# Layer 0's rounds: one bounded product of factors for the decays in six of eight rounds, and dt's chain taken apart over a slot

## The chip, the cores and the metric

The kernel runs on one core of a Trainium2 chip. The core has a matrix engine (TensorE, PE in the profile; its weight loads are listed as PEld), a vector engine (VectorE, DVE), a scalar engine for activations (ScalarE, ACT), a general one (GpSimd, POOL) and queues for DMAs (here mostly SyncE's, SP). Each engine executes its instructions in order; an instruction waits on semaphores for what it needs from other engines. The metric is the device time in microseconds, the median of several runs.

## The reference, cut to what matters

The kernel computes four layers on an input of 8 sequences x 512 tokens x 128 features. Only the mixer of layer 0 is touched. It is a selective state-space recurrence whose inputs depend on the step before:

```python
def step(carry, inp):
    state, y_prev = carry
    xBC_t, dt_t, z_t = inp
    xBC = silu(xBC_t + y_prev @ W_rxbc.T)
    dtr = silu(dt_t + y_prev @ W_rdt.T)
    ...
    dt = jax.nn.softplus(dtr + dt_bias).astype(jnp.float32)
    dA = jnp.exp(dt * A)
    ...
    state = state * dA[:, :, None, None] + dt[:, :, None, None] * x_h[:, :, :, None] * B_hn[:, :, None, :]
    y = (state * C_hn[:, :, None, :]).sum(-1) + D_param[None, :, None] * x_h
    y = y.reshape(B, D_SSM)
    g = y * silu(z_t)
    ...
    yn = (gg * jax.lax.rsqrt(ms + EPS)).reshape(B, D_SSM) * norm_w
    out_t = yn @ W_out.T
    return ((state, yn), out_t)
```

There are 4 heads of 64 features, and the state is 128 wide. `A` is negative, so each step lets the state decay by `exp(dt * A)`. Layer 0 also has an expert network (8 experts, each for all tokens, one chosen per token); it does not depend on the mixer.

## The kernel before, in words

**Rounds.** The step's dependence on `y_prev` is resolved by iteration: `ROUNDS` = 8 times the whole sequence is computed in parallel from the last round's `yn`. A round of one sequence is a `Unit` (k, b), so there are 64 units, k outermost. A unit has four tiles c of 128 tokens. In round 0 the raw inputs come from the convolution (16 matmul passes a tile, L157, and z, L166); they are stored to DRAM (`xd`, and z as `zd`) and fetched again in later rounds (L141, L146), where the feedback product (8 passes, L161) is added (L169). After the last round, `apart_still` compares rounds 6 and 7 (largest difference against 5e-5, `CLOSE`); if they differ by more, a loop over `again` computes more rounds, each unit by itself. In the profiled execution that loop is not entered: L169 runs 224 times, 7 rounds of 8 units of 4 tiles.

**Slots.** `run` writes the order out by hand under a manual schedule, and each engine keeps that order. Slot i works on four units at once: `new` (unit i, its inputs), `mid` (unit i-1, silu, dt, the turn of B and C and their pair products), `old` (unit i-2, products, outputs) and `last` (unit i-3, its last output and its norm). There are 67 slots of four chunks. Two calls of `fill` in each chunk add expert work: one of them usually four hidden matmuls (`ph`, L609, then four Relus on ACT, L622), the other four output matmuls (`po`, L591, then an add on DVE one call later, L630). Their number per chunk does not depend on the units.

**One unit.** At the start of a slot, ACT loads the silu table (L126), does one silu over all four tiles (L176), and loads the table with exp and ln. Then comes dt's chain: v and nv on DVE (L192, L193), exp on ACT (L194), e1 (L195), ln (L196), and d, l, dt, da (L197 to L200). PE forms running sums and totals of da (L203, L204), and ACT their exponentials `ec`. For the decays between two tokens of a tile, POOL multiplies the triangle by da for each head (`span`, L211, 128x512), PE sums over it (`pseg`, L225), ACT takes the exponential (`E`, L229), and DVE multiplies it with the masked pair products `gm` to `M` (L253, L234). PE then needs four products a tile, one for each head's own `M` (L260), the part from the carried state (L262) and, but for the last tile, the tile's own state (L265). POOL also makes `xdt`, `xp` and `xw` (L219, L221, L237). DVE forms the state and the outputs (L275 to L291); ACT squares them for the norm (L292); PE turns them (L298) and ACT copies them to `gT` (L299), which feeds the next round.

**PSUM.** There are pools of one bank or two: `pre`, a shared tile "b" (pc, pbc, pz and pr take turns in it), `pseg`, `py`, and a shared tile "s" (pds and pgt); two more banks are the experts'.

Of the kernel before, what the change touches and what calls it, by code (L numbers as in the profile page):

```python
# [55 lines left out]

CW = 516
HW = CW // 2
ROUNDS = 8
CLOSE = 5e-5  # L60
SILU, EXPLN = "silu_and_others", "natural_log_exp_and_others"


class Unit:
    def __init__(self, k, b):
        self.k, self.b = k, b
        self.bc, self.gm, self.xd, self.xp, self.e, self.m, self.r = {}, {}, {}, {}, {}, {}, {}
        self.py, self.ps, self.s = {}, {}, {}


class Recurrence:

# [3 lines left out]
    def __init__(self, tc, ctx, keep, K, I, dr, xnT, spare, B, T):  # L76
# [5 lines left out]
        self.psA, self.psB, self.psG = pool("pa", 1, space=PSUM), pool("pb", 1, space=PSUM), pool("pg", 1, space=PSUM)  # L82
        self.psY, self.psS = pool("py", 1, space=PSUM), pool("ps", 1, space=PSUM)
# [13 lines left out]
        tri = load("tri", [P, 4, P])  # L97
        self.upto, self.after, self.shift, self.carry = (tri[:, i, :] for i in range(4))
# [9 lines left out]
        WcT = self.un.tile([P, 4, CW], F32, name="ux")[:, 0, :]  # L108
# [4 lines left out]
        self.spare = spare  # L113
# [6 lines left out]
        self.apart = wp.tile([P, B], F32, name="apart")  # L120
        self.xd = [dr.tile([P, 4, CW], F32, name=f"xd{b}") for b in range(B)]
        self.zd = [dr.tile([P, 4, 256], F32, name=f"zd{b}") for b in range(B)]
        self.yd = [dr.tile([P, 4, 256], F32, name=f"yd{b}") for b in range(B)]
# [14 lines left out]
    def fetch(self, u):  # L138
        u.x = self.un.tile([P, 4, CW], F32, name="ux")
        for c in range(self.NC if u.k else 0):  # L140
            self.nc.sync.dma_start(out=u.x[:, c, :], in_=self.xd[u.b][:, c, :])  # L141

    def fetch_gate(self, u):
        u.z = self.un.tile([P, 4, 256], F32, name="uz")
        if u.k:
            self.nc.sync.dma_start(out=u.z, in_=self.zd[u.b])  # L146

    def inputs(self, u, c):

        nc = self.nc  # L150
        pre = self.psA.tile([P, 2, 512], F32, name="pre")
# [10 lines left out]
        x = self.halves(u.x[:, c, :])  # L162
        if u.k == 0:
            nc.vector.tensor_tensor(x, pre[:, :, 0:HW], self.halves(self.convb), ALU.add)
            pz = self.psB.tile([P, 512], F32, name="pz", tag="b")
            nc.tensor.matmul(pz[:, 0:256], self.xnT[:, u.b, c * P + 3 : c * P + 3 + P], self.WzT, start=True, stop=True)  # L166
            nc.vector.tensor_copy(u.z[:, c, :], pz[:, 0:256])
        else:
            nc.vector.scalar_tensor_tensor(x, pre[:, :, 0:HW], self.rs[:, u.b, c : c + 1], x, ALU.mult, ALU.add)  # L169

    def silu(self, u):
        nc = self.nc
        if u.k == 0:
            nc.sync.dma_start(out=self.xd[u.b], in_=u.x)
        self.tables(SILU)
        nc.scalar.activation(u.x, u.x, AF.Silu)  # L176
        if u.k == 0:
            nc.scalar.activation(u.z, u.z, AF.Silu)
            nc.sync.dma_start(out=self.zd[u.b], in_=u.z)
        self.tables(EXPLN)  # L180

    def small(self, name, n=4):
        return self.sm.tile([P, 4, n], F32, name=name)

    def dt(self, u):

        nc = self.nc
        tt, stt = nc.vector.tensor_tensor, nc.vector.scalar_tensor_tensor
        four = lambda t: t.rearrange("p (c h) -> p c h", c=4)
# [18 lines left out]
    def spans(self, u, c):  # L208

        u.r[c] = self.wk.tile([P, 4, P], F32, name="span")  # L210
        self.nc.gpsimd.tensor_tensor(  # L211
            u.r[c], self.upto.unsqueeze(1).to_broadcast([P, 4, P]), u.da[:, c, :].unsqueeze(2).to_broadcast([P, 4, P]), ALU.mult
        )
# [203 lines left out]

# [1089 lines left out]
```

## Time and profile before

| what | value |
|---|---|
| runs of the kernel before | 4888.32, 4879.22, 4885.47 us; median 4885.47 us |
| the profiled execution: its time | 4862.31 us |
| its span, first to last instruction | 4860.5 us |
| mean granted TensorE clock | 0.911 |
| busy over the span | PE 3921.8 us (81%), DVE 2433.7, ACT 2148.3, POOL 1682.9 us |
| first matmul of layer 0's rounds (L157) | at 77.27 us |
| last matmul of the last unit's norm (L312) | at 2880.81 us |
| sums of da (L203) of slots 1, 3, 8, 49, 51, 59, 64 | at 115.57, 201.59, 444.75, 2123.92, 2206.04, 2561.06, 2804.69 us |

The times of L203 mark the slots, since it stands once at the start of each. Slots 3 to 7 take 48.6 us on average ((444.75 - 201.59) / 5), slots 8 to 48 take 40.96, slots 51 to 58 take 44.4, slots 59 to 63 take 48.7 us. In the rows of the timeline below, the first number is the start, the second the duration in us; a pair of brackets holds the idle time of the engine before it and what ended it. A matmul of fp32 shows as two records, and its duration contains the pipeline's latency, so the work of a group is read from one start to the next.

### The profile page before, as it was taken

Reading aid. Unit: us, or ns where it says so; the run is one execution under the profiler, and the core shown is the slowest. Engines: PE = TensorE matmul, PEld = TensorE weight load, DVE = VectorE, ACT = ScalarE, POOL = GpSimd, SP = SyncE. Lnnn points to the kernel's source line nnn. Section 1 sums busy time; section 2 is a strip of 40 time slices with the busy share of each in tenths; the row PEclk is TensorE's granted clock in tenths of the full one; section 3 lists DMA queues with packets and bytes.
Section 4 is the critical chain, followed back from the end, with each engine's and each line's share of the span. In section 5 each row is a group of like instructions: output and inputs, shape, how many; then the busy total and the mean of one; then the engine's idle time right before and its main releaser. Section 6 shows DMA issues by size and latency. Waiting matters only on the chain. (4 is left out here: it accounts for less than half of the span.)

```text
span 4860.5 us, 74671 instructions
## 1 busy us (share of the span) xinstructions
PE 3921.8 (81%) x27702; PEld 2869.4 (59%) x27702; DVE 2433.7 (50%) x7179; ACT 2148.3 (44%) x5067; POOL 1682.9 (35%) x2097
## 2 busy tenths in 40 slices
PE   6877777777777777777777766769999897999998
PEld 5666666666666666666565554225555555666666
DVE  4334444444444444444444545647777336777781
ACT  1333444444444444443333323336666224666675
POOL 1222333333333333332332331630000345777782
PEclk7999999999999999998888888769999898999999
DMA  3001111111111111111111113100000510000000
GB/s 105 36 31 48 44 40 42 42 40 44 40 39 43 35 37 41 39 44 48 53 59 40 51 31 69 52 0 2 2 2 2 106 36 21 2 2 2 2 2 18
DMA packets 85732, 169.07 MB, mean 35 GB/s; under 512 B 10860, under 2 KB 28528, under 8 KB 84210
## 3 DMA queue, kind: packets, MB, share of 16 engines
q1 hardware_dynamic: 80796, 160.22, 11.0%
q8 instruction: 223, 3.65, 0.3%
q10 hardware_dynamic: 4566, 3.99, 0.3%
q14 instruction: 147, 1.20, 0.1%
HBM read 139.50 MB, written 24.68 MB: 34 GB/s over the span
## 5 line engine op out<-in xcount | busy, mean ns | idle before, releaser
L253 DVE TENSOR_TENSOR gm<-pbc,w_tri 128x128 f32<-128x128 f32 x256 | 74.7, 292 | 1002.2 <-PE pbc L251 1002.2
L237 POOL TENSOR_TENSOR xw<-xdt,E 128x256 f32<-128x256 f32 x192 | 119.4, 622 | 1302.6 <-ACT E L229 1295.0
L622 ACT ACTIVATE hid<-ph,be 128x128 f32<-128x128 f32 x1024 | 291.9, 368 | 578.0 <-PE ph L609 578.0
L1196 POOL TENSOR_SCALAR gp<-toe,ng 128x207 f32<-128x207 f32 (+1 forms) x512 | 490.8, 967 | 107.0 <-DVE mn L885 73.0
L898 PE MATMUL pt<-ident,sb 128*128 128x128 f32 x3328 | 497.3, 283 | 13.3 <-ACT pT L901 8.6
L161 PEld LDWEIGHTS pre<-w_Wr,gT 128*128 128x128 f32 x1792 | 378.0, 211 | 190.7 <-issue 141.0
L898 PEld LDWEIGHTS pt<-ident,sb 128*128 128x128 f32 x3328 | 356.2, 141 | 208.8 <-ACT pT L903 78.6
L161 PE MATMUL pre<-w_Wr,gT 128*128 128x258 f32 x1792 | 468.4, 408 | 0.0
L885 DVE CUSTOM_DVE_ANT_0 sb<-ps_s,gp 128x512 f32<-128x512 f32 x512 | 324.1, 685 | 100.5 <-PE ps_s L877 82.8
L901 ACT COPY pT<-pt 128x512 f32<-128x512 f32 (+3 forms) x512 | 255.5, 499 | 243.5 <-PE pt L898 242.1
L229 ACT ACTIVATE E<-pseg 128x512 f32<-128x512 f32 x256 | 152.9, 597 | 451.9 <-PE pseg L225 451.9
L211 POOL TENSOR_TENSOR span<-w_tri,da 128x512 f32<-128x512 f32 x256 | 276.8, 1082 | 217.2 <-PE pseg L225 145.4
L891 ACT ACTIVATE sb<-sb,mn 128x512 f32<-128x512 f32 (+3 forms) x512 | 330.5, 646 | 21.9 <-DVE mn L885 16.5
L225 PE MATMUL pseg<-span,w_tri 128*128 128x512 f32 x512 | 332.6, 737 | 0.0
L591 PE MATMUL po<-ew,hid 128*128 128x128 f32 x2048 | 284.5, 284 | 58.3 <-DVE xn L630 58.3
L203 PE MATMUL pc<-da,w_tri 128*128 128x16 f32 x128 | 38.9, 384 | 354.5 <-DVE da L200 354.5
L591 PEld LDWEIGHTS po<-ew,hid 128*128 128x128 f32 x2048 | 261.5, 200 | 62.0 <-DVE xn L630 61.3
L609 PEld LDWEIGHTS ph<-x,ew 128*128 128x128 f32 x2048 | 279.0, 198 | 15.5 <-ACT hid L622 1.2
L169 DVE SCALAR_TENSOR_TENSOR ux<-pre,rs,ux 128x516 f32<-128x516 f32 x224 | 168.1, 750 | 237.2 <-PE pre L161 237.2
L609 PE MATMUL ph<-x,ew 128*128 128x128 f32 x2048 | 280.2, 282 | 1.0 <-ACT hid L622 1.0
L292 ACT ACTIVATE y<-g 128x256 f32<-128x256 f32 x256 | 106.2, 415 | 361.6 <-DVE g L291 361.6
L260 PE MATMUL py<-xdt,M 128*128 128x64 f32 x2048 | 264.7, 273 | 0.0
(343 smaller groups left out, 8211.2 us busy)
## 6 DMA issues: line engine op xcount, KB each, us to landing
ux<-xd SPq DMA_DIRECT2D x224, 258.0 KB, 3.9
uz<-zd SPq DMA_DIRECT2D x56, 512.0 KB, 5.6
cB<-dc SPq DMA_DIRECT2D x16, 1024.0 KB, 14.1
xd<-ux SPq DMA_DIRECT2D x8, 1032.0 KB
wu<-in_f_up_dram SPq DMA_DIRECT2D x9, 512.0 KB
wd<-in_f_down_dram SPq DMA_DIRECT2D x9, 512.0 KB, 4.2
x<-in_u_dram SPq DMA_DIRECT2D x16, 256.0 KB, 5.3
zd<-uz SPq DMA_DIRECT2D x8, 512.0 KB, 2.6
```

Of the source, the lines that this page charges most:

```text
L161: nc.tensor.matmul(pre[:, h, 0:HW], g, self.W[:, f, cols], start=(f == 0), stop=(f == 1))
L211: self.nc.gpsimd.tensor_tensor(u.r[c], self.upto.unsqueeze(1).to_broadcast([P, 4, P]), u.da[:, c, :].unsqueeze(2).to_broadcast([P, 4, P]), ...
L225: self.nc.tensor.matmul(pg.rearrange("p h t -> p (h t)"), self.after, u.r.pop(c).rearrange("p h t -> p (h t)"), start=True, stop=True)
L260: nc.tensor.matmul(py[:, 0, 64 * h : 64 * h + 64], m[:, h, :], u.xd[c][:, h, :], start=True, stop=True)
L591: self.nc.tensor.matmul(self.po[:, r], hid[:, f, :], w2[:, f, :], start=(f == 0), stop=(f == 3))
L609: self.nc.tensor.matmul(self.ph[:, f, :], self.w[n][0][:, f * P : (f + 1) * P], self.xhT[:, i * P : (i + 1) * P], start=True, stop=True)
L622: self.nc.scalar.activation(self.hid[n][:, f, :], self.ph[:, f, :], AF.Relu, bias=self.be[:, self.jobs[n][0], f : f + 1])
L885: nc.vector.tensor_tensor_reduce(out=sb[:, 0:L], in0=ps[:, g, 0:L], in1=bias[g], scale=1.0, scalar=3.0e38, op0=ALU.add, op1=ALU.min, accum ...
L891: nc.scalar.activation(sb[:, 0:L], sb[:, 0:L], AF.Exp, scale=-1.0, bias=mn)
L898: nc.tensor.transpose(pt[:, j * P : (j + 1) * P], sb[:, j * P : (j + 1) * P], self.ident)
L901: nc.scalar.copy(t[:, 0:L], pt[:, 0:L])
L1196: nc.gpsimd.tensor_scalar(t[:, k0:k1], toe[:, h, o : o + k1 - k0], gates[b][:, i, h : h + 1], None, ALU.mult)
```

## The change

Six rounds (k below `EXACT` = 6) no longer build a matrix of decays for each head. They use two factors for each token instead: `exp` of the sum of da since the middle of the tile, and its inverse. The sums are made with two new matrices, `mid` (the triangle less one half) and `halves_` (one half everywhere); da is bounded at -16 and the sums at 72 either way (`STEEP`, `FAR`). The inverse factor and dt are multiplied onto x (`xs`), the factor onto the gate z (`zf`), and one matmul for all heads with the bare `gm` replaces four; the state's product accumulates into the same PSUM columns. `span`, `pseg`, `E`, `M` and `xw` are then not made. Rounds 6 and 7 keep the sums of their own.

In all rounds, the silu is done tile by tile from the second chunk of the slot before (the third where `mid` is exact), with the table loads there and at the slot's start. dt's chain is split (`dt_begin`, `dt_log`, `dt_end`, `sums`, `factors`) over the first two chunks. The products of `old` open a chunk, and the fetches go tile by tile. D and the gate are multiplied once in round 0 (`dz`, stored and fetched like z), so that an output is one product and one sum. B and C are copied from PSUM by one instruction. The scaling of rounds 6 and 7 for the comparison goes from DVE to POOL; the comparison is of squares summed over a token's 256 features against `CLOSE` squared, one ACT instruction a tile. If it fails, 10 rounds of `again` start from nothing. The PSUM tiles are allocated once, and several results share a bank (`pb`, `pt`, and by turns `py` and `pg`).

In the cut diff below only the added lines are shown, but for the first two; what they take the place of are the functions of the same names in the kernel above, and `dt`, which is split.

```diff
-ROUNDS = 8
+ROUNDS, EXACT = 8, 6
 CLOSE = 5e-5
+STEEP, FAR = -16.0, 72.0
...
+        self.pre = ps.tile([P, 2, 512], F32, name="pre")
+        self.pb, self.pt, self.py, self.pg = (ps.tile([P, 512], F32, name=n) for n in ("pbc", "pt", "py", "pseg"))
...
+        self.upto, self.after, self.shift, self.carry, self.mid, self.halves_ = (tri[:, i, :] for i in range(6))
...
+    def fetch(self, u, c):
+        if u.k:
+            self.nc.sync.dma_start(out=self.ux[u.n % 3][:, c, :], in_=self.xd[u.b][:, c, :])
     def fetch_gate(self, u):
+        u.dz = self.un.tile([P, 4, 256], F32, name="dz", bufs=2)
         if u.k:
+            u.z = self.un.tile([P, 4, 256], F32, name="uz")
             self.nc.sync.dma_start(out=u.z, in_=self.zd[u.b])
+            self.nc.sync.dma_start(out=u.dz, in_=self.dzd[u.b])
...
+    def collect(self, u, c):
+        nc = self.nc
+        pre = self.pre[:, :, 0:HW]
+        if u.k == 0:
+            u.raw = self.wk.tile([P, CW], F32, name="span")
+            nc.vector.tensor_tensor(self.halves(u.raw), pre, self.halves(self.convb), ALU.add)
+            nc.sync.dma_start(out=self.xd[u.b][:, c, :], in_=u.raw)
+            nc.vector.tensor_copy(u.z[:, c, :], self.pt[:, 256:512])
         else:
+            x = self.halves(u.x[:, c, :])
+            nc.vector.scalar_tensor_tensor(x, pre, self.rs[:, u.b, c : c + 1], x, ALU.mult, ALU.add)
+            u.raw = u.x[:, c, :]
+    def silu(self, u, c):
+        nc = self.nc
+        nc.scalar.activation(u.x[:, c, :], u.raw if u.k == 0 else u.x[:, c, :], AF.Silu)
...
+    def skip(self, u, c):
         if u.k == 0:
...
+            self.nc.gpsimd.tensor_tensor(u.dz[:, c, :], u.z[:, c, :], self.Dx, ALU.mult)
+            if c == self.NC - 1:
+                self.nc.sync.dma_start(out=self.dzd[u.b], in_=u.dz)
...
+    def dt_begin(self, u):
+        nc = self.nc
+        u.v, u.nv, u.ex = (self.small(n) for n in ("v", "nv", "ex"))
+        four = lambda t: t.rearrange("p (c h) -> p c h", c=4)
+        nc.vector.tensor_tensor(four(u.v), u.x[:, :, 256:260], four(self.dtb), ALU.add)
+        nc.vector.scalar_tensor_tensor(u.nv, u.v, -1.0, u.v, ALU.mult, ALU.min)
+        nc.scalar.activation(u.ex, u.nv, AF.Exp)
...
+    def dt_log(self, u):
+        nc = self.nc
+        u.e1, u.l = self.small("e1"), self.small("l")
+        nc.vector.tensor_scalar(u.e1, u.ex, 1.0, None, ALU.add)
+        nc.scalar.activation(u.l, u.e1, AF.Ln)
...
+    def dt_end(self, u):
         nc = self.nc
         tt, stt = nc.vector.tensor_tensor, nc.vector.scalar_tensor_tensor
...
+        d = self.small("d")
+        u.dt, u.da = self.small("dt"), self.small("da", bufs=3)
+        stt(d, u.e1, -1.0, u.ex, ALU.add, ALU.subtract)
+        tt(u.l, u.l, d, ALU.subtract)
+        stt(u.dt, u.v, 0.0, u.l, ALU.max, ALU.add)
+        tt(u.da, u.dt, self.A, ALU.mult)
+        if not u.exact:
+            nc.vector.tensor_scalar(u.da, u.da, STEEP, None, ALU.max)
+    def sums(self, u):
+        nc = self.nc
+        pc = u.pc = self.pb[:, 384:432]
+        for i, w in enumerate((self.upto, self.K["ones"], self.after) if u.exact else (self.mid, self.halves_)):
+            nc.tensor.matmul(pc[:, 16 * i : 16 * i + 16], w, u.da, start=True, stop=True)
...
+    def factors(self, u):
+        nc = self.nc
+        u.ec, w = self.small("ec", 48, bufs=3), self.small("w")
+        u.bd = self.small("bd", bufs=3)
+        if u.exact:
+            nc.scalar.activation(u.ec, u.pc, AF.Exp)
+            nc.vector.tensor_tensor(u.bd, u.ec[:, 32:48], u.dt, ALU.mult)
+            return
+        cl = self.small("cl", 32)
+        nc.vector.tensor_scalar(cl, u.pc[:, 0:32], FAR, -FAR, ALU.min, ALU.max)
+        nc.scalar.activation(u.ec[:, 0:32], cl, AF.Exp)
+        nc.scalar.activation(w, cl[:, 0:16], AF.Exp, scale=-1.0)
+        nc.vector.tensor_tensor(u.bd, w, u.dt, ALU.mult)
...
+    def scaled(self, u, c):
+        tt = self.nc.gpsimd.tensor_tensor
+        x = u.x[:, c, 0:256]
+        t = lambda name: self.wk.tile([P, 256], F32, name=name, bufs=2)
+        four = slice(4 * c, 4 * c + 4)
+        u.xs[c] = t("xs")
+        tt(self.heads(u.xs[c]), self.heads(x), self.over((u.dt if u.exact else u.bd)[:, four]), ALU.mult)
+        if not u.exact:
+            u.zf[c] = t("zf")
+            tt(self.heads(u.zf[c]), self.heads(u.z[:, c, :]), self.rate(u, 0, c), ALU.mult)
+        elif c + 1 < self.NC:
+            u.xw[c] = t("zf")
+            tt(self.heads(u.xw[c]), self.heads(x), self.over(u.bd[:, four]), ALU.mult)
+        u.xz[c] = t("xz")
+        tt(u.xz[c], x, u.dz[:, c, :], ALU.mult)
     def spans(self, u, c):
...
+        if u.exact:
+            u.r[c] = r = self.wk.tile([P, CW], F32, name="span")[:, 0:512].rearrange("p (h t) -> p h t", h=4)
+            da = u.da[:, 4 * c : 4 * c + 4].unsqueeze(2).to_broadcast([P, 4, P])
+            self.nc.gpsimd.tensor_tensor(r, self.upto.unsqueeze(1).to_broadcast([P, 4, P]), da, ALU.mult)
     def decays(self, u, c):
...
+        if u.exact:
+            self.nc.tensor.matmul(self.pg, self.after, u.r.pop(c).rearrange("p h t -> p (h t)"), start=True, stop=True)
+            u.m[c] = self.taps[:, c, 0:512]
+            self.nc.scalar.activation(u.m[c], self.pg, AF.Exp)
     def weighted(self, u, c):
...
+        if u.exact:
+            m = u.m[c].rearrange("p (h t) -> p h t", h=4)
+            self.nc.vector.tensor_tensor(m, m, u.gm.pop(c).unsqueeze(1).to_broadcast([P, 4, P]), ALU.mult)
...
+    def turn(self, u, c):
+        nc = self.nc
+        for i in range(2):
+            nc.tensor.transpose(self.pb[:, i * P : (i + 1) * P], u.x[:, c, 260 + i * P : 260 + (i + 1) * P], self.K["ident"])
+        u.bc[c] = self.wk.tile([P, 256], F32, name="bc", bufs=5)
+        nc.scalar.copy(u.bc[c], self.pb[:, 0:256])
...
+    def pairs(self, u, c):
+        nc = self.nc
+        nc.tensor.matmul(self.pb[:, 256:384], u.bc[c][:, 0:P], u.bc[c][:, P:256], start=True, stop=True)
...
+    def masked(self, u, c):
+        u.gm[c] = self.wk.tile([P, P], F32, name="gm", bufs=5)
+        self.nc.vector.tensor_tensor(u.gm[c], self.pb[:, 256:384], self.upto, ALU.mult)
...
+    def products(self, u, c):
+        nc = self.nc
+        cT = u.bc.pop(c)[:, P:256]
+        xs = u.xs.pop(c)
+        bank = self.py if u.exact or c % 2 == 0 else self.pg
+        u.py[c], u.ps[c] = bank, (self.pt[:, 256:512] if u.exact else bank[:, 256:512])
         if c + 1 < self.NC:
...
+            nc.tensor.matmul(u.ps[c], u.x[:, c, 260:388], u.xw.pop(c) if u.exact else xs, start=True, stop=True)
+        if u.exact:
+            m = u.m.pop(c)
+            for h in range(4):
+                e = slice(64 * h, 64 * h + 64)
+                nc.tensor.matmul(bank[:, e], m[:, h * P : h * P + P], xs[:, e], start=True, stop=True)
+            if c:
+                nc.tensor.matmul(bank[:, 256:512], cT, u.s[c], start=True, stop=True)
+            return
+        nc.tensor.matmul(bank[:, 0:256], u.gm.pop(c), xs, start=True, stop=(c == 0))
         if c:
+            nc.tensor.matmul(bank[:, 0:256], cT, u.s[c], start=False, stop=True)
+    def state(self, u, c):
+        if c + 1 == self.NC:
+            return
...
+        u.s[c + 1] = s = self.wk.tile([P, 256], F32, name="S", bufs=2)
+        if u.exact:
...
+        if c:
+            tt(s, u.s[c], ps, ALU.add)
+        tt(heads(s), heads(s if c else ps), self.rate(u, 1, c), ALU.mult)
+        tt(heads(s), heads(s), self.rate(u, 1, c + 1), ALU.mult)
+    def outputs(self, u, c):
...
+        bank = u.py.pop(c)
         y = self.wk.tile([P, 256], F32, name="y", bufs=2)
+        if not u.exact:
...
+            tt(y, bank[:, 0:256], u.zf.pop(c), ALU.mult)
         else:
...
+            if c:
+                tt(self.heads(y), self.heads(bank[:, 256:512]), self.rate(u, 0, c), ALU.mult)
+                tt(y, y, bank[:, 0:256], ALU.add)
+            tt(y, y if c else bank[:, 0:256], u.z[:, c, :], ALU.mult)
+        tt(u.g[:, c, :], y, u.xz.pop(c), ALU.add)
...
+    def norm(self, u):
+        nc = self.nc
+        pr = self.pb[:, 448:452]
...
+        if u.k >= EXACT:
+            self.root(self.rt[:, u.b, :], u.ms[:, 1:5])
+            for c in range(self.NC):
+                rt = self.rt[:, u.b, c : c + 1].to_broadcast([P, 256])
+                nc.gpsimd.tensor_tensor(self.yn[:, c, :], u.g[:, c, :], rt, ALU.mult)
+            if u.k > EXACT:
+                self.compare(u)
+            nc.sync.dma_start(out=self.yd[u.b], in_=self.yn)
...
+    def recall(self, u):
+        if u.k > EXACT:
+            self.nc.sync.dma_start(out=self.was, in_=self.yd[u.b])
...
+    def compare(self, u):
+        nc = self.nc
         for c in range(self.NC):
...
+            w = self.was[:, c, :]
+            nc.vector.tensor_tensor(w, w, self.yn[:, c, :], ALU.subtract)
+            nc.scalar.activation(w, w, AF.Square, accum_out=self.apart[:, u.b, c : c + 1])
...
+            new, mid, old, last, nxt = at(i), at(i - 1), at(i - 2), at(i - 3), at(i + 1)
+            tile = lambda c: (old, c) if c < NC else (mid, c - NC)
             if mid:
+                self.fetch_gate(mid)
+                self.tables(EXPLN)
+                self.dt_begin(mid)
+            ready = []
             for c in range(NC):
                 was, cw = (old, c - 1) if c else (last, NC - 1)
+                if old:
+                    self.products(old, c)
+                    self.state(old, c)
+                    if nxt:
+                        self.fetch(nxt, c)
+                elif nxt:
+                    self.fetch(nxt, c)
+                if c == 1 and mid:
+                    self.sums(mid)
+                if mid:
+                    self.turn(mid, c)
+                if c == 0 and mid:
+                    self.dt_log(mid)
+                if was:
+                    self.keep(was, cw)
+                if old:
+                    self.outputs(old, c)
+                if c == 0 and mid:
+                    self.dt_end(mid)
+                if c == 1:
+                    if mid:
+                        self.factors(mid)
+                    if last:
+                        self.norm(last)
+                if c == 2 and old:
+                    self.recall(old)
+                if new:
+                    self.inputs(new, c)
+                if c < 2 and old:
+                    self.decays(old, c + 2)
+                if c in (1, 2) and mid:
+                    self.decays(mid, c - 1)
+                fill(0)
+                if mid:
+                    self.pairs(mid, c)
+                if new:
+                    self.collect(new, c)
+                    ready.append(c)
+                if mid:
+                    self.masked(mid, c)
+                if c >= 2 and mid:
+                    self.weighted(mid, c - 2)
+                if c < 2 and old:
+                    self.weighted(old, c + 2)
+                if c == (2 if mid and mid.exact else 1) and new:
+                    self.tables(SILU)
+                if c >= (2 if mid and mid.exact else 1):
+                    while ready:
+                        self.silu(new, ready.pop(0))
+                fill(1)
+                if mid:
+                    self.skip(mid, c)
+                    self.spans(mid, c)
+                u1, c1 = tile(c + 1)
                 if u1:
                     self.scaled(u1, c1)
...
+    def close(self):
+        nc = self.nc
+        ok = self.small("ok", 32)
+        nc.vector.tensor_scalar(ok, self.apart.rearrange("p b c -> p (b c)"), CLOSE * CLOSE, None, ALU.is_le)
+        far = self.small("far", 1)
+        nc.vector.tensor_reduce(out=far, in_=ok, op=ALU.min, axis=AX.X)
+        nc.tensor.transpose(self.pb[0:1, 0:P], far, self.K["ident"])
         flag = self.sm.tile([1, 1], mybir.dt.int32, name="flag")
...
+        nc.vector.tensor_reduce(out=flag, in_=self.pb[0:1, 0:P], op=ALU.min, axis=AX.X)
         return nc.values_load(flag[0:1, 0:1], min_val=0, max_val=1)
...
+    def further(self):
+        nc, more = self.nc, ROUNDS + 2
+        with self.tc.If(self.close() < 1):
+            nc.vector.memset(self.gT, 0.0)
+            nc.vector.memset(self.rs, 1.0)
+            with self.tc.For_i(0, more, 1):
+                self.again()
+            with self.tc.If(self.close() < 1):
+                with self.tc.For_i(0, self.T - more, 1):
+                    self.again()
```

## The prediction, made before the change was run

> **What bounds the kernel now.** I read the page's slices first. The rounds fill the first 2.9 ms, and no engine is at its limit there. The table by stages gives the steady stretch, slots 8 to 50; its columns are the stretch, its length, then busy time and instructions of PE, PEld, DVE, ACT and POOL, the granted clock, the DMA share and GB/s:
>
> ```profile
> 444.75:2206.04 1761.29, 1329.96 (x7740) 1090.79 (x7741) 728.79 (x1893) 719.95 (x1978) 546.85 (x688) 0.92 0.13 41
> ```
>
> Over 43 slots that is 40.96 us a slot, with PE busy for 30.9, DVE 16.9, ACT 16.7, POOL 12.7. So PE has the most work, but 10 us of each slot are lost on it. The timeline of PE over one slot shows where:
>
> ```profile
> 1012.13 0.49 PE L251 MATMUL pbc<-cT,bT 128*128 128x128 f32 x2 [0.44 <-ACT cT L247]
> 1018.01 0.61 PE L203 MATMUL pc<-da,w_tri 128*128 128x16 f32 x2 [5.39 <-DVE da L200]
> 1018.46 0.59 PE L204 MATMUL pc<-da,ones 128*128 128x16 f32 x2
> 1018.89 2.06 PE L225 MATMUL pseg<-span,w_tri 128*128 128x512 f32 x2
> 1020.73 2.57 PE L161 MATMUL pre<-w_Wr,gT 128*128 128x258 f32 x8
> ...
> 1027.62 1.02 PE L225 MATMUL pseg<-span,w_tri 128*128 128x512 f32 x2
> 1028.48 1.90 PE L161 MATMUL pre<-w_Wr,gT 128*128 128x258 f32 x8
> 1030.22 0.38 PE L298 MATMUL pgt<-ident,g 128*128 128x128 f32 x2
> 1030.44 0.28 PE L311 MATMUL pr<-ms,w_tri 128*128 128x4 f32 x2
> 1030.58 0.36 PE L312 MATMUL pr<-ms,w_tri 128*128 128x4 f32 x2
> 1030.80 1.08 PE L260 MATMUL py<-xdt,M 128*128 128x64 f32 x8
> 1031.72 0.65 PE L262 MATMUL py<-S,cT 128*128 128x256 f32 x2
> 1032.21 0.59 PE L265 MATMUL pds<-xw,ux 128*128 128x256 f32 x2
> 1032.64 1.05 PE L609 MATMUL ph<-x,ew 128*128 128x128 f32 x8
> 1033.53 0.38 PE L244 MATMUL pbc<-ident,ux 128*128 128x128 f32 x2
> 1033.75 1.06 PE L591 MATMUL po<-ew,hid 128*128 128x128 f32 x8
> 1035.25 0.49 PE L251 MATMUL pbc<-cT,bT 128*128 128x128 f32 x2 [0.44 <-ACT cT L247]
> 1035.57 1.02 PE L225 MATMUL pseg<-span,w_tri 128*128 128x512 f32 x2
> ```
>
> The 5.39 us wait comes once a slot. After it PE is slow: pc, pseg and pre start 0.45, 0.43, 1.84 and about 2.4 us apart, against 0.36 (for pr), 0.86 and 1.74 later, some 2.2 us. The list of waits for 600 to 2000 us gives two more, pgt for g (97.8 us) and pbc for cT (60.4 us), over 34 slots 4.6 us a slot. Together 12.2; what is left is the work itself, about 28 us. The rows of ACT and DVE show why da is late: a table load, one long silu, a second load, then a chain in which each step waits:
>
> ```profile
> 1012.09 1.28 ACT L126 ACT_TABLE_LOAD   x1
> 1013.39 1.92 ACT L176 ACTIVATE ux<-ux 128x2064 f32<-128x2064 f32 x1
> 1015.33 1.28 ACT L126 ACT_TABLE_LOAD   x1
> 1016.62 0.22 ACT L194 ACTIVATE e<-nv 128x16 f32<-128x16 f32 x1
> 1017.78 0.17 DVE L200 TENSOR_TENSOR da<-dt,w_Al 128x16 f32<-128x16 f32 x1
> ```
>
> **PE's work after, slots 8 to 48.** From starts above, a chunk of `old`'s round below 6 has pds 0.43, one py of 256 columns (as L262) 0.49, the carried part 0.49, turn 0.22, keep 0.22, inputs 1.74, ph 0.89, pairs 0.32 and po 0.89: 5.69. Chunk 0 has no carried part, chunk 3 no pds; chunk 1 has sums (two like L311 and L312, 0.36) and the norm 0.36. 4 x 5.69 - 0.92 + 0.72 = 22.6 us a slot. What goes is pseg (4 x 0.86) and half of py (4 x 0.43).
>
> **Does anything else now set the slot?** ACT: copy of B and C 0.37 (as L299), gT 0.37, square 0.60, Relus 1.14, silu of a tile about 0.6 (as E, 512 columns): 3.1 a chunk, with two loads and four small exponentials 15.9. DVE: 8 state and 8 output operations at 0.42 to 0.6, collect 3.0, gm 1.2, adds 1.4, ten small ones 2.0: 15 to 17. POOL: three products a tile at 0.62 to 0.83 and a root of 1.0: 9.5. All are under 22.6, so order decides. I laid the slot out from its first product (time 0). ACT finishes the last silu at 0.6, the load at 1.9, exp at 2.1, B and C at 2.5, ln at 2.7; da stands at 4.4. PE needs B and C for pairs at 4.0 and da for sums at 6.6: dt's chain is covered by chunk 0. If it were not, its old price is 5.4 plus 2.2 us a slot. Silus of two tiles and the load end 2.5 us into chunk 2, ahead of its pairs. Scaling, now three POOL operations, is one chunk ahead.
>
> One wait may be new. norm's sums are queued on PE behind `factors`, whose read of pc on DVE stands behind state and outputs; both are in the tile `pb`. If a write to one region waits for a read of another, PE stands from 7.4 to 9.4, 2.0 us, and inputs, fill and pairs behind it. The trace doesn't show regions of one tile; its nearest row is turn's wait for z's copy in the shared tile (0.25 us, L244 for L167 in round 0). Bounds 0 and 2.0; I take 2.0, since that row has a wait for other contents of one bank. With 0.4 for waits such as pbc's 0.44: **25.0 us** a slot. The clock: the steady 0.92 holds the slow stretches; where PE is densest (4300 to 4600 us, 296.6 of 300 busy) it is 1.00, so I use the full-speed starts. At 0.92, 22.6 would be 24.6.
>
> The Trainium skill (ScalarE: Activation LUTs, "What ACT_TABLE_LOAD costs") gives a switch 1.28 us of load plus about 1.38 of drain. Here the silu starts 0.02 us after the load ends. By the page ACT would carry 18.7 us a slot and da would stand at 5.8; the sum would be the same.
>
> **The other slots.** Slots 3 to 7 (round 0) add 8 passes of pre, 1.74, and z 0.43 a chunk: 25 + 8.7 = 33.7. Slot 0 changes little (PE ends at 108); slots 1 and 2 need 27 and 31.5, so slot 3 starts at 167. In slots 50 on, the exact unit has pseg and four py again: 22.6 + 3.4 + 1.6 + 0.2 = 27.8. Added waits: norm behind the exponential of pc on ACT 2.3; pseg used twice in chunk 1, 0.7; xw behind span on POOL 0.3: 31. Slots 51 to 58: two roots (2 x 1.01), four scalings (0.7 each) and a span precede xs and xw on POOL, 1.5 more: 32.5. Slots 59 to 63: the comparison on DVE and its four squares on ACT wait for these scalings, and `E` behind them, about 4 more: 36. Slot 49 is mixed, 27. The tail loses its dt wait and the old comparison on DVE (76.5 to 62).
>
> DMAs: dz adds one of 512 KB a slot to SP, 2.06 MB a slot or 82 GB/s at 25 us. The queue gave 105 GB/s in the page's first slice, and uz lands in 5.6 us against the 18 until it is read; nothing, or, uncovered, 5.6 us a slot. Setup, one larger table (0.13 MB), nothing.
>
> **Sum.** To slot 3: 201.6 - 167 = 35. Slots 3 to 7: 243.2 - 168.5 = 75. 8 to 48: 1679.2 - 41 x 25 = 654. 49 and 50: 82.1 - 58 = 24. 51 to 58: 355.0 - 260 = 95. 59 to 63: 243.6 - 180 = 64. Tail 14. Together 961 us. The profiled execution's 4862.3 us becomes 3901; its median of three runs is 23 above it, so 4885.5 becomes about **3925**.
>
> **Rivals.**
> *PE still waits each slot.* For: ACT has two loads and 14 us of other work between silu and da, and one late Relu moves everything behind it. Against: the layout has 1.5 to 2 us to spare at pairs and sums. Price 7.6 us on slots 3 to 48, 46 x 7.6 = 350: 4275.
> *Exact slots gain nothing.* Slots 49 to 63 stay as before, through POOL's longer queue: 183 back, 4110. Against: PE waits 5.4 there too.
> *The rounds don't close and the loop runs; slower.* Place: `further`. 10 more rounds are 80 units, each by itself. Bounds for a unit: PE's 27.8 less the experts' 7.1, 20.7 us; or three slots of before, 123. The nearest row is the last unit's way alone, from its table load (2802.0) to its root (2883.4) with inputs about 10: 91. 80 x 91 = 7280, so 11,200 us (5580 to 13,800). In double precision the reference's inputs give half sums up to 68.6 (bound 72) and da under -16 for 0.02% of the values, so the bounds hardly act. Largest row differences of the last three rounds: 1.05e-3, 1.5e-4, 1.36e-5, limit 5e-5. With random relative errors of 3e-6 on each factor in the first six rounds the last becomes 1.6e-5, with 1e-5 it is 5.4e-5: it decides at about 9e-6. No row shows the error of an exponential here.
>
> The skill's page (ScalarE: Activation LUTs, "Precision budgets") gives exp a mean error of 25 ULP and a largest of 165, by my estimate 2e-6 and 1.5e-5: mostly inside, with tokens outside. No run here shows it.
>
> **Chances.** Forecast 0.60, PE still waits 0.18, exact slots 0.13, the loop 0.09. The forecast's own low end takes out the 2.0 and 2.3 us waits (48 x 2.0 + 15 x 2.3 = 130) and the 0.4s: 3775. The range goes on to the exact rival and part of the first: 3760 to 4150. About 0.2% is what measurement can tell from none: faster 0.90, same 0.01, slower 0.09.
>
> **What would show it.** Slots of 23 to 25 us between sums' matmuls, no PE wait over 3 us before them, pseg only in rounds 6 and 7; PE's clock near 1 in the steady slots. norm's first matmul waiting on DVE would show the `pb` wait. xs or xw ahead of products would show POOL. Any work of `again` would show the loop. I am wrong if PE has regular waits on ACT at pairs, or if slots 59 to 63 exceed 45 us.

## The result, and the profile after: the rounds run as forecast, and then a loop of 2843 us

The changed kernel takes 6778.32 us (median of 4 runs, 6768.81 to 6780.13) against 4882.35 us for the kernel before beside it (4877.81 to 4888.32): a ratio of 1.3878, 95% interval 1.3854 to 1.3902. It is slower, where 3925 us was forecast.

The table by stages of the changed kernel, in the columns of the prediction's first fence: slots 8 to 48, slots 51 to 58, slots 59 to the end of the last norm, and what comes between two transposes of line L524, which `close` issues:

```profile
344.86:1359.91 1015.05, 937.18 (x6070) 853.31 (x6069) 552.88 (x1639) 588.88 (x1722) 362.58 (x537) 0.98 0.28 89
1423.97:1690.12 266.15, 239.19 (x1458) 199.69 (x1456) 149.14 (x368) 132.67 (x360) 134.76 (x168) 0.96 0.25 83
1690.12:1935.98 245.86, 193.10 (x1137) 162.13 (x1135) 133.97 (x313) 112.36 (x336) 109.28 (x136) 0.88 0.22 76
1942.73:4785.63 2842.90, 2143.80 (x9442) 1554.12 (x9442) 1586.42 (x3685) 1723.89 (x3411) 1322.76 (x1680) 0.83 0.26 89
```

The first three rows are the rounds. Slots 8 to 48 take 1015.05 / 41 = 24.8 us each, with PE busy for 22.9 of it; before it was 40.96 and 30.9. The rounds end at 1935.98 us, where those of before ended at 2880.81. The fourth row is `further`: its first `close` finds that the rounds have not closed and runs `again` 10 x 8 times; its second `close` is content. The groups of instructions say the same. `bd` is multiplied at L251 only for an exact unit, and there are 16 of these in the rounds:

```profile
L251 DVE TENSOR_TENSOR bd<-ec,dt x96: 161/176/282, 1363.0 to 4752.9; 128x16 f32<-128x16 f32 x96
```

96 is 16 and 80 more. Without the 2842.9 us the profiled execution would have taken 6777.9 - 2842.9 = 3935 us. So the question is not where time went inside the rounds but why they did not close.

PE over the start of a slot of the changed kernel, to be held against the 5.39 us wait of before:

```profile
716.68 0.51 PE L243 MATMUL pbc<-da,w_tri 128*128 128x16 f32 x4
...
719.25 0.39 PE L388 MATMUL pbc<-ms,w_tri 128*128 128x4 f32 x2 [1.56 <-DVE cl L254]
...
719.71 1.99 PE L178 MATMUL pre<-w_Wr,gT 128*128 128x258 f32 x8
```

The sums of da (L243) start with no bracket, so da is there in time. The one long wait that comes in every slot is that of norm's first product for the read of pc, as the prediction had it, at 1.56 us instead of 2.0. A short one stands beside it: the experts' output product (L708) waits 0.33 us for DVE, 13.3 us in slots 8 to 48.

### The profile page after: what moved, and what is told of

Same layout as the page of the kernel before. It is cut to its first block, busy times and chain, and to the rows that moved or that the text cites. A ratio compares the mean times of both kernels' runs of the same rounds, so it can differ in the third digit from the quotient of the medians.

```text
span 6776.1 us, 103298 instructions
## 1 busy us (share of the span) xinstructions
PE 5647.3 (83%) x35639; PEld 4182.8 (62%) x35639; DVE 3831.9 (57%) x10640; ACT 3773.0 (56%) x8357; POOL 2890.5 (43%) x3729
## 3 DMA queue, kind: packets, MB, share of 16 engines
q1 hardware_dynamic: 186780, 450.46, 20.7%
## 5 line engine op out<-in xcount | busy, mean ns | idle before, releaser
L178 PE MATMUL pre<-w_Wr,gT 128*128 128x258 f32 x4352 | 1219.4, 416 | 273.4 <-DVE ux L193 181.5
L178 PEld LDWEIGHTS pre<-w_Wr,gT 128*128 128x128 f32 x4352 | 828.7, 205 | 456.7 <-DVE ux L193 256.2
L193 DVE SCALAR_TENSOR_TENSOR ux<-pre,rs,ux 128x516 f32<-128x516 f32 x544 | 408.6, 751 | 379.6 <-PE pre L178 353.5
L276 POOL TENSOR_TENSOR xz<-ux,dz 128x256 f32<-128x256 f32 x576 | 445.4, 774 | 390.9 <-DVE g L369 179.5
L326 PEld LDWEIGHTS py<-xs,taps 128*128 128x128 f32 x3072 | 465.4, 222 | 137.6 <-issue 71.9
L286 PE MATMUL pseg<-span,w_tri 128*128 128x512 f32 x768 | 455.0, 678 | 74.0 <-ACT taps L288 63.3
L1015 PE MATMUL pt<-ident,sb 128*128 128x128 f32 x3328 | 501.4, 285 | 13.3 <-ACT pT L1018 8.5
L326 PE MATMUL py<-xs,taps 128*128 128x64 f32 x3072 | 475.8, 302 | 39.7 <-DVE taps L293 38.7
L268 POOL TENSOR_TENSOR xs<-ux,dt 128x256 f32<-128x256 f32 x384 | 246.2, 641 | 585.6 <-PE py L326 388.7
L198 ACT ACTIVATE ux<-ux 128x516 f32<-128x516 f32 x544 | 338.2, 634 | 80.0 <-issue 32.1
L408 DVE TENSOR_TENSOR s<-s 128x256 f32<-128x256 f32 x352 | 264.6, 809 | 200.8 <-POOL s L395 200.8
L288 ACT ACTIVATE taps<-pseg 128x512 f32<-128x512 f32 x384 | 229.1, 597 | 221.0 <-PE py L326 110.6
```

Source lines behind the costliest of these rows:

```text
L178: nc.tensor.matmul(pre[:, h, 0:HW], g, self.W[:, f, cols], start=(f == 0), stop=(f == 1))
L193: nc.vector.scalar_tensor_tensor(x, pre, self.rs[:, u.b, c : c + 1], x, ALU.mult, ALU.add)
L198: nc.scalar.activation(u.x[:, c, :], u.raw if u.k == 0 else u.x[:, c, :], AF.Silu)
L276: tt(u.xz[c], x, u.dz[:, c, :], ALU.mult)
L286: self.nc.tensor.matmul(self.pg, self.after, u.r.pop(c).rearrange("p h t -> p (h t)"), start=True, stop=True)
L326: nc.tensor.matmul(bank[:, e], m[:, h * P : h * P + P], xs[:, e], start=True, stop=True)
```

## Experiments

### One look at each suspicion

Four kernels ran side by side. **e1_noloop** only puts the loop out of reach:

```diff
-CLOSE = 5e-5
+CLOSE = 1.0
```

> The limit of the comparison is 1.0 instead of 5e-5, so the further rounds never run; all else is the changed kernel. Theory (the loop is the whole loss): 6778 less the 2843 us between the two reads of the comparison, 3935 us, 0.806 of before. Rival (the rounds themselves lose too, or the loop's presence hides a cost elsewhere): over 4100 us.

Measured: 3923.71 us (3921.22 to 3935.73), ratio to before 0.8057 (0.8035 to 0.8079). Line L251 shows x16. The loop is the whole of the loss, and the rounds alone are worth what the forecast said, 3925.

**e2_ladder** reads how far the last two rounds are apart. It puts in place of the further rounds a row of comparisons; each limit that is exceeded issues a memset whose width is the limit's number:

```diff
+    def ladder(self, src, limits, width):
...
+        for i in range(len(limits)):
+            v = nc.values_load(flags[0:1, i : i + 1], min_val=0, max_val=1)
+            with self.tc.If(v < 1):
+                nc.vector.memset(mark[:, 0 : width + i + 1], 0.0)
...
+        norms = [1e-5, 2e-5, 3e-5, 5e-5, 7e-5, 1e-4, 2e-4, 4e-4, 1e-3]
+        self.ladder(self.apart.rearrange("p b c -> p (b c)"), [n * n for n in norms], 100)
+        self.ladder(self.most.rearrange("p b c -> p (b c)"), [3e-6, 1e-5, 2e-5, 3e-5, 5e-5, 7e-5, 1e-4, 2e-4, 1e-3], 200)
```

> The further rounds are left out. In their place stand ladders: for each of a row of limits, a memset of its own width runs only if the largest value is above the limit. Values: the row norm of the difference of rounds 6 and 7 (the changed kernel's measure), its largest element (the measure of before), in round 5 for two sequences the product of a factor and its inverse less one, and the sum over the triangle less half the total less the centred sum, which is 0 without rounding. Theory A (the exponentials' error): row norm 5e-5 to 2e-4, product off by 1e-5 to 4e-5, sums off by under 1e-5. Rival B (the sums' rounding): sums off by over 1e-5, product off by under 3e-6. Rival C (only the measure is stricter): largest element under 5e-5 while the row norm is over it. Time about 4000 us.

Measured: 3961.42 us. The last memset of each of the first two ladders, from DVE's timeline:

```profile
1951.93 0.15 DVE L550 MEMSET ux<- 128x106 f32 x1 [0.53 <-DVE ux L550]
...
1960.24 0.23 DVE L550 MEMSET ux<- 128x207 f32 x1 [0.46 <-DVE ux L550]
```

106 is the sixth limit of the row norm, 207 the seventh of the largest element. So both lie between 1e-4 and 2e-4, and `CLOSE` asks for 5e-5. The two ladders on the factors (of round 5, first two sequences) end at 304 and 402: the product of a factor and its inverse is off from 1 by 2e-5 to 4e-5 at the worst token, and the sums of the two halves differ by 3e-6 to 1e-5. The prediction's rival decided at a random error of about 9e-6 on each factor, so by itself this run seemed to bear it out.

**e3_exact7** and **e4_exact3** take factors away: only round 0 has them in the one, rounds 0 to 4 in the other.

```diff
-Unit(k, b, k * self.B + b, k >= EXACT)
+Unit(k, b, k * self.B + b, k >= 1)
```

> Only round 0 takes the factors; rounds 1 to 7 have their own sums; the comparison and the further rounds are as changed. Theory A or B (the factors make the difference): it closes, 3935 + 40 slots x 8.3 = 4270 us. Rival D (the comparison itself is at fault, or its rounding noise is above the limit): the loop runs, 4270 + 2843 = 7110 us.

> Rounds 5, 6 and 7 have their own sums, five rounds take the factors; comparison and further rounds as changed. If a round shrinks the factors' error to about a tenth, as double precision shows, it closes: 3935 + 8 x 8.3 = 4000 us. If the error does not shrink that way, the loop runs: 6845 us.

Measured: 7099.0 us (7084.33 to 7104.09), ratio 1.456 (1.4524 to 1.4595), and 6844.8 us (6842.71 to 6845.43), ratio 1.4045 (1.4016 to 1.4074). L251 shows x136 and x104, 80 more than the exact units of the rounds (56 and 24): the loop runs in both. Seven rounds without a factor do not close either. That contradicts the prediction's cause.

### Does the distance depend on the factors at all?

**e5_exact7_ladder** and **e6_exact3_ladder** put the first two ladders into those kernels. **e7_nine_exact3_ladder** and **e8_nine_exact8_ladder** run nine rounds, the first six with factors or only the first:

```diff
-ROUNDS, EXACT = 8, 6
+ROUNDS, EXACT = 9, 7
```

> As the run with seven rounds of own sums, but with the two ladders (row norm and largest element of the difference of rounds 6 and 7) in place of the further rounds, which are left out. Theory E (the stricter measure: without factors the iteration itself ends between the two measures): row norm over 5e-5, at most 1e-4; largest element at most 5e-5, which before's limit lets pass. Rival D (the comparison in the slots is at fault, for example it reads a wrong array): both over 1e-4, as with the factors. Double precision alone would give 1.4e-5 and 6e-6.

> Rounds 5, 6 and 7 with own sums, two ladders, further rounds left out. Theory E with the factors' error shrunk to a tenth by the extra round: the same two rungs as with seven such rounds (row norm 5e-5 to 1e-4, largest element at most 5e-5). Rival D: both over 1e-4.

> Nine rounds, the first six with factors, the last three with own sums; ladders on the difference of rounds 7 and 8; further rounds left out. If the iteration shrinks the difference to about a tenth a round: row norm at most 2e-5. If the exponentials' steps set a floor: 3e-5 to 1e-4. Time 3924 + 8 slots x 33 + 30 for the ladders, 4220 us.

> Nine rounds, all but round 0 with own sums; ladders on the difference of rounds 7 and 8; further rounds left out. Plain shrinking: row norm at most 1e-5. A floor that does not come from the factors: the same rung as in the run before, 3e-5 to 1e-4. Rival D: over 1e-4.

Measured: e5 and e6 end at 128x106 and 128x207 like e2 (4256.45 and 4016.82 us). e7 and e8 (4188.44 and 4503.28 us) show only the first limit of each ladder; e8's whole answer is

```profile
2507.31 0.14 DVE L544 MEMSET ux<- 128x101 f32 x1 [0.33 <-issue]
2514.75 0.23 DVE L544 MEMSET ux<- 128x201 f32 x1 [0.24 <-issue]
```

that is, a row norm of 1e-5 to 2e-5 and a largest element of 3e-6 to 1e-5. By their expectations e5 and e6 came out as rival D had it, a fault of the comparison itself; e7 and e8, where D asked for over 1e-4 again, speak against it. Neither of the two figures given for e8's row norm (at most 1e-5, or 3e-5 to 1e-4) was met. One round with factors or six make no difference on the ladder, and one more round brings the distance down at least fivefold. The double-precision rounds of the prediction stand at 1.36e-5 at the eighth round; the chip has this at the ninth. The kernel is one round behind, and what is common to all these kernels is round 0.

### Round 0: which raw rows does the silu read?

`collect` leaves the raw inputs of a tile under the single name `u.raw`, and `silu` reads that name in round 0. In the kernel before one silu took all four tiles from `u.x`. Now `run` collects tiles 0 and 1 before it empties `ready` at c == 1. The timelines of DVE and of ACT in the changed kernel show the order, for the first unit of round 0:

```profile
85.42 0.70 DVE L188 TENSOR_TENSOR span<-pre,convb 128x516 f32<-128x516 f32 x1 [4.37 <-PE pre L174]
91.78 0.70 DVE L188 TENSOR_TENSOR span<-pre,convb 128x516 f32<-128x516 f32 x1 [2.99 <-PE pre L174]
```

```profile
93.24 1.28 ACT L133 ACT_TABLE_LOAD   x1
94.53 0.63 ACT L198 ACTIVATE ux<-span 128x516 f32<-128x516 f32 x1
95.38 0.62 ACT L198 ACTIVATE ux<-span 128x516 f32<-128x516 f32 x1
```

Two collects, then two silus. A profile leaves buffer numbers out, so it can't show that both silus read the second span; the code says so. Tile 0 of every sequence starts from tile 1's raw inputs. What goes to DRAM (`xd`) is right, so later rounds mend it and cost no more than a late start. I put that slip into the reference's rounds in double precision: the distance of rounds 6 and 7 becomes 1.76e-4 as a row norm and 1.06e-4 as the largest element (without it 1.35e-5 and 5.7e-6), and a ninth round has 1.0e-5 and 6.7e-6. All four lie on the rungs measured, the 1.0e-5 at the very edge of its rung. This could be tried directly.

**e9_own_raw** keeps the raw inputs per tile, **e10_own_raw_ladder** has the ladders besides, and **e12_before_ladder** has them in the kernel before:

```diff
-            u.raw = self.wk.tile([P, CW], F32, name="span")
+            u.raw = u.raws[c] = self.wk.tile([P, CW], F32, name="span")
...
-        nc.scalar.activation(u.x[:, c, :], u.raw if u.k == 0 else u.x[:, c, :], AF.Silu)
+        nc.scalar.activation(u.x[:, c, :], u.raws[c] if u.k == 0 else u.x[:, c, :], AF.Silu)
```

> The changed kernel with one change: the raw inputs that collect leaves for silu in round 0 are kept per tile (u.raws[c]) instead of under one name. In the changed kernel's round 0, collect runs for tiles 0 and 1 before the first silu of the slot, so the silu of tile 0 reads the name after tile 1 has written it: tile 0 of every sequence starts from tile 1's raw inputs. Theory 'wrong start' (a wrong tile 0 in round 0 costs about one round of convergence; the reference's rounds in double precision with that slip put in give a difference of rounds 6 and 7 of 1.76e-4 as a row norm and 1.06e-4 as the largest element, without it 1.35e-5 and 5.7e-6): the rounds close, the loop doesn't run, 3924 us (3910 to 3940) as with the loop put out of reach, line L251 shows x16. Rival 'wrong start and factors' (without the slip the factors' own error still keeps a row above 5e-5): the loop runs, about 6770 us, x96. Rival 'not the start' (the rounds close for another reason too slowly): 6770 us as well, told apart by the ladder of the next run.

> As the run with a raw input per tile, with the ladders in place of the further rounds: the loop is left out whatever the comparison gives. Theory 'wrong start': row norm above 1e-5 and at most 2e-5 or 3e-5, largest element between 3e-6 and 2e-5 (each at least one rung, by a factor of 5 to 10, below the 1e-4 to 2e-4 of the four ladders with the slip and eight rounds). Theory 'wrong start and factors': row norm above 5e-5. Rival 'not the start': both unchanged at 1e-4 to 2e-4. Time about 3960 us, as the first ladder run (3961).

> The kernel before, with ladders on its own comparison (its largest element, and row norms added) in place of its further rounds, which are left out. Theory 'wrong start': the kernel before has no slip and no factors, so its eighth round differs from the seventh by the double precision 1.35e-5 (row norm, rungs 1e-5 to 2e-5) and 5.7e-6 (largest element, rungs 3e-6 to 1e-5). Rival 'the chip converges more slowly than double precision in any case': 5e-5 or more in the row norm. Time 4885 plus some 30 to 40 us for the ladders.

Measured: e9 takes 3929.04 us (5 runs, 3924.24 to 3940.8), ratio 0.8052 (0.8033 to 0.807). Its line L251 shows x16, and after the transpose of `close` PE goes on to the output projection (L580):

```profile
1937.02 0.37 PE L524 MATMUL pbc<-ident,far 128*1 128x128 f32 x1 [6.74 <-DVE far L523]
1943.09 12.01 PE L580 MATMUL pout<-w_WoT,gT 128*128 128x128 f32 x80 [5.70 <-PEq L532]
```

e10 (3976.13 us) ends its first two ladders at the second limit:

```profile
1953.57 0.14 DVE L550 MEMSET ux<- 128x102 f32 x1 [0.57 <-DVE ux L550]
...
1960.97 0.23 DVE L550 MEMSET ux<- 128x202 f32 x1 [0.80 <-DVE ux L550]
```

The row norm is 2e-5 to 3e-5 and the largest element 1e-5 to 2e-5, inside the expectation. e12 (4885.43 us) shows 128x101 and 128x201 alone: the kernel before stands at 1e-5 to 2e-5 and 3e-6 to 1e-5. Its ladders did not show in its one time, against 30 to 40 us expected. So the rounds close as soon as round 0 starts right. The row norm of e10 is 1 to 3 times that of e12 by the ends of their rungs, and 1.5 to 2.2 times the 1.35e-5 of double precision. That this is the price of the factors is likely but not shown: no run has a right round 0 and no factors, and e10 differs from e12 in more than the factors. A factor of 1.7 to 2.5 is left below 5e-5.

### The wait in the shared bank

**e11_early_norm** is e9 with norm's two products issued right behind the sums, where nothing in `pb` is being read:

```diff
                 if c == 1 and mid:
                     self.sums(mid)
+                if c == 1 and last:
+                    self.norm_sums(last)
...
     def norm(self, u):
         nc = self.nc
-        pr = self.pb[:, 448:452]
-        nc.tensor.matmul(pr, self.shift, u.ms[:, 1:5], start=True, stop=False)
-        nc.tensor.matmul(pr, self.carry, u.ms[:, 0:4], start=False, stop=True)
-        self.root(self.rs[:, u.b, :], pr)
+        self.root(self.rs[:, u.b, :], self.pb[:, 448:452])
```

`norm_sums` holds the two products that left `norm`.

> As the run with a raw input per tile, and the two products of norm(last) (L388, L389) issued right behind the sums of mid in slot part 1, ahead of turn, instead of behind the read of the sums by the factors; what reads them stays where it was. Tests the wait at L388 that the prediction put at 2.0 us a slot and the trace shows at 1.56 (steady) and 1.60 (exact) with TensorE otherwise without a gap. Theory 'the wait is the path': the waiting goes and nothing takes its place, 1.56 x 41 + 1.60 x 16 + some of slots 3 to 7 = about 90 to 95 us less than the run beside it (3830). Rival 'VectorE would be late anyway' (the chain from sums through dt's factors to the scaled rows on GpSimd and the products of the next slot sets the pace): less than 30 us saved, and a gap of the same size appears before L321 or L330.

Measured: 3828.37 us (5 runs, 3816.02 to 3836.96), ratio to before 0.7841 (0.782 to 0.7863), and 100.7 us less than e9 in the same batch. The group of L388 in e9 and then in e11; behind the bar stand busy time, mean ns, and the idle time before it with what ended it:

```profile
L388 PE MATMUL pbc<-ms,w_tri 128*128 128x4 f32 x128 | 24.5, 262 | 98.3 <-DVE cl L254 72.0 <-ACT ec L250 26.3
```

```profile
L388 PE MATMUL pbc<-ms,w_tri 128*128 128x4 f32 x128 | 23.1, 251 | 0.0
```

All 98.3 us of this wait are gone, and the time is 100.7 us shorter. That the two agree so well is chance, as the stages show. Slots 8 to 48 and slots 51 to 58, of e9 and then of e11, in the columns of the tables above:

```profile
340.04:1356.82 1016.78, 938.82 (x6069) 854.78 (x6068) 552.89 (x1639) 589.25 (x1722) 362.61 (x537) 0.98 0.28 89
1419.20:1683.20 264.00, 236.26 (x1458) 198.26 (x1457) 148.72 (x368) 132.61 (x360) 134.74 (x168) 0.97 0.25 84
```

```profile
323.31:1264.28 940.97, 924.35 (x6070) 843.82 (x6069) 563.83 (x1639) 585.10 (x1722) 376.36 (x537) 1.00 0.30 96
1321.05:1587.86 266.81, 236.34 (x1458) 201.37 (x1456) 147.72 (x368) 132.91 (x360) 135.14 (x168) 0.96 0.25 83
```

In slots 8 to 48 the wait was 64.2 us, and 75.8 us were saved, because the granted clock rose as well. In e9 the clock stands at half for 3.41 us in 11 of these 41 slots, which last about 26.0 us; most of the others last 24.35. In e11 it never does, and nearly all slots last 22.91 us. PE is then busy for 924 of 941 us: the steady rounds are bound by PE's own work.

In slots 51 to 58 the wait was 12.8 us, and nothing was saved. There PE now waits longer for the scaled rows that POOL makes (`xw`, in a tile named zf). The row of the list of waits in this stretch, of e9 and then of e11, gives us in total, times, and the longest:

```profile
PE pt L321 <- POOL zf L274: 8.9, 11, 0.8
```

```profile
PE pt L321 <- POOL zf L274: 25.0, 16, 2.3
```

So the expectation's rival, with its gap before L321, holds in these slots. In slots 59 to 63 the wait of 8.4 us went and 4.4 us were saved, since PE's wait for the exponential of the decays (L286) grew from 22.9 to 31.1 us. e11 is the best of the versions: 21.6% under the time of before.

## Why the prediction was wrong, and where it was right

**What failed is the rival "the rounds don't close and the loop runs".** It named the right place, `further`, and gave it .09; the sum has nothing for it, and 2842.9 us were measured. That chance came from one cause, the relative error of the factors, weighed against the 9e-6 at which it decides. The runs showed another. Without factors in seven rounds the loop still ran (e3), and with all factors and a right round 0 it did not (e9). The prediction followed when each silu runs, tile by tile, and what it costs. It did not follow which buffer each one reads, and so took the start of the iteration as unchanged. In the runs tile 0 started wrong, and the rounds were one behind (e8 against e2). `collect` and `silu` stand a few lines apart in the diff. Moving the silu behind a second `collect` is the very reordering whose price was worked out.

**The price of that rival** was 11,200 us, 91 us a unit, taken from one unit's way alone. Measured: 2842.9 / 80 = 35.5 us a unit. "Each by itself" was wrong, since in the loop the next unit's inputs run before this one's sums. At the start of a pass, PE's timeline shows seven tiles' inputs (L178, four to a unit) ahead of the first sums (L243), of which the first and the last are shown:

```profile
3086.19 3.80 PE L178 MATMUL pre<-w_Wr,gT 128*128 128x258 f32 x8 [8.93 <-PEq L535]
...
3106.85 2.01 PE L178 MATMUL pre<-w_Wr,gT 128*128 128x258 f32 x8 [0.85 <-DVE ux L193]
3108.69 0.29 PE L243 MATMUL pbc<-da,w_tri 128*128 128x16 f32 x2
```

PE's own work in a unit is 2143.8 / 80 = 26.8 us, so the lower bound of 20.7, made of PE's work alone, was the better guide.

**The sum of the rounds held.** Forecast 3925 us; with the loop out of reach 3923.71, with round 0 mended 3929.04. By its terms:

| term | forecast, us | changed kernel, us |
|---|---|---|
| slot 3 starts at | 167 | 175.5 |
| slots 3 to 7, each | 33.7 | 33.9 |
| slots 8 to 48, each | 25.0 | 24.8 |
| of that, PE's work | 22.6 | 22.9 |
| the wait in `pb`, steady | 2.0 | 1.56 |
| the same behind the exponential, exact | 2.3 | 1.60 |
| slots 49 and 50 together | 58 | 64.1 |
| slots 51 to 58, each | 32.5 | 33.3 |
| slots 59 to 63, each | 36 | 37.8 |
| from slot 64's sums to the last norm | 62 | 56.8 |

The misses up to slot 3 (8.5 us), in slots 49 and 50 (6.1) and in the exact ones (8 x 0.8 and 5 x 1.8) are partly balanced by the steady slots (10 us in all) and the tail (5.2). By these terms the rounds should have ended at 1920 us; they ended at 1935.98, 16 us late. The sum for the profiled execution, 3901, was low against the profiled 3924.87 of e1 and 3929.04 of e9; the 23 us that the forecast added for the median of the kernel before made up for it by chance. dt's chain is covered, as the layout of the slot said: the sums wait for nothing. So "PE still waits each slot" (.18) and "exact slots gain nothing" (.13) are both out. The wait in `pb` was given bounds of 0 and 2.0 and taken at 2.0; e11 shows that it was real and on the path of the steady slots. The low end of the range also took 2.3 us off each exact slot; in slots 51 to 58 the wait was worth nothing, because POOL's scaling was due at about the same time.

**The clock** was taken at full speed because PE is dense. Granted were 0.98 in slots 8 to 48 (0.92 before) and 0.83 in the loop, where PE is busy for 75%.

**The rule on table loads** (the Trainium skill, ScalarE: Activation LUTs, "What ACT_TABLE_LOAD costs") adds a drain of about 1.38 us to each load. After the change the silu starts 0.01 us after the 1.28 us load ends (93.24 + 1.28, 94.53 above), as before the change, where it was 0.02 us. The measurement decides: no such drain stands between load and silu here.

**The rule on precision** (the same page, "Precision budgets") gave my estimates of 2e-6 and 1.5e-5 for the exponential's error. The product of two exponentials was off by 2e-5 to 4e-5 at worst (e2), which agrees with twice the larger estimate, 3e-5. Where the mean lies no run showed.

What stays open: how near to 5e-5 other inputs would bring the version with factors. Only these inputs were run.

## What to carry to other kernels

When a kernel iterates until a comparison is content, a change has two prices: that of an iteration, and that of one iteration more. The second can hang on a value that no time in the profile shows, so when a producer and its consumer are moved apart, write down for each name how many of its values are alive at once, and which one each reader gets. And a product for one purpose that shares a bank with a read for another should be issued where no read is under way: two small matmuls moved by a few instructions gave 2.6% here. What a wait is worth is read stage by stage: where another engine is due just behind it, taking it away gave nothing.

## What the hardware showed that I had not expected

The granted TensorE clock was higher where PE had fewer gaps: 0.98 with PE busy for 92% of the steady slots, 1.00 with 98% (e11), and 0.92 with 76% in the steady slots of before. The figures are means of two values. In the steady slots of before, the profile has 6.83 us at half clock about once a slot of 40.96 us, and one such stretch (1015.24 to 1022.07) begins inside the 5.39 us wait shown in the prediction; in slots 8 to 48 of e9 it has 3.41 us about every fourth slot, and in those of e11 none. The busy share alone doesn't set it, for the loop has 0.83 at 75%; what does, no run here isolates.

In the loop, where the order is not written by hand and two units overlap, ACT loads a table 610 times for 80 units (L198 260, L288 190, L225 80, L250 50, L219 30); at 1.283 us each that is 783 us, 9.8 us a unit, against two loads a slot in the rounds. And a conditional on a value read back costs little where it decides once: in e2 one rung of the ladder follows the other by 0.68 us (1951.25 to 1951.93, with its memset), and in e9 6.07 us pass from the transpose of `close` to the first matmul behind it.
